# Attention scores and a token gather over three bfloat16 pieces in place of float32, with the exponentials one unit further behind

## The chip, the cores and the metric

The kernel runs on one core of a Trainium2 chip. The metric is the device time of one execution in microseconds (us), as the median of several runs. The core has five engines that run at the same time and wait for each other through semaphores: TensorE (PE in the profile; its weight loads are shown apart as PEld), VectorE (DVE), ScalarE (ACT), GpSimd (POOL) and SyncE (SP), which here only issues DMAs.

## The reference: what is computed

The input is x with 4 batches of 512 tokens of 128 numbers. In turn:

1. x = x + 0.5 * ffn(layernorm(x)), where ffn is a causal latent attention with 16 heads of 8 numbers, followed by a mixture of 8 experts of which 2 count for each token.
2. x = x + attention(layernorm(x)), a full (not causal) attention with 16 heads of 8 numbers.
3. Step 1 once more.
4. x = x + 0.5 * chosen(layernorm(x)): for each of 8 experts the 64 tokens with the highest gate are gathered, attend to each other with rotated positions, and are added back.
5. Four layers of additive attention with a feed-forward part, then step 4 once more.

Steps 1 to 3 are the "first layer" of the kernel. The scores of its attention are

```
scores = einsum('bhnd,bhmd->bhnm', q * scale, k)
attn = softmax(scores)
```

with only 8 numbers per head to sum over. All data are float32.

## The kernel before, in words

**Layout of the scores.** The attention of the first layer is 12 tasks: 3 parts (causal, full, causal) by 4 batches. A task keeps q and k transposed, spread over partitions so that a row group of 32 partitions (called j, 0 to 3) holds one head at every fourth partition, with 4 head groups g along the free dimension: tiles qA and kA (L240, L241), two of each, used in turn. A product of q's and k's rows of one row group sums over 32 partitions, of which 8 carry data. Partition 1 of every row group in kA is -1 and in qA is the maximum of that token's scores, so that the second product yields scores already less their maximum.

**Units.** A task is cut in units: a unit is a bank-wide (512 columns) piece of scores for one head group, 16 units in a full task and 10 in a causal one (there some units are made of two shorter pieces, 384+128 or 256+256 columns). There are 144 units. A unit is worked in two halves of two row groups each.

**Stages of a unit.** `maxima` (L522) multiplies q by k for tokens as rows; `reduce_max` (L536) takes the row maximum on VectorE (L543 with the causal mask, L547 without). When the last unit of a head group is reduced, `place_maxima` (L549) transposes the maxima on VectorE (L551) and puts them in qA's partition 1 by four DMAs (L555). GAP units later `shifted` (L557) multiplies k by q the other way round, `exponent` (L571) takes the exponential on ScalarE (L574), `mask` (L576) clears the upper triangle on GpSimd for causal tasks, and LAG units after that `products` (L590) multiplies by the values (L605).

**Order of the work.** The loop at L628 writes the order by hand. At step n it issues the maxima of unit n, the shifted scores of the unit that `behind` names (five units behind at first, FIRST; six after unit 26, HOLD and GAP at L22 and L23), the products two units later, and beside them one expert's `hidden` (L460) and one `combined` (L477) of the mixture, and one step of background work: the preparation of the next task (L301), its placing (L383), the ends of older ones. `bank` and `clock` (L53) choose a PSUM bank by planned times. A scheduler below this may still reorder what is independent.

**Preparing and placing a task.** `prepare` ends with q in qC (L346) and k in kC (L351), float32, 128 partitions by 512. `spread` (L354) copies both into qA and kA by one DMA each (for the first task by four each on two queues). It may run only when the task before last no longer reads the same buffers: L388 waits for the last unit of that task plus GAP.

**The gather.** `choice` (L778) computes the gates of two batches, finds the 64 highest per expert in eight rounds on VectorE (L836, L838), and leaves for each batch the token rows yg (the 128 normalised numbers, the rotation's cosines and sines, the place and the gates: 201 columns) and the slot numbers byt. `chosen_attention` (L858) builds a 0/1 matrix `pick` (L869) and multiplies it with yg (L880), 16 products per batch, which gathers the rows. It runs twice, after the first layer and after the additive layers; each time the choice for batches 2 and 3 runs while batches 0 and 1 are already attended to.

Of the kernel before, what the change touches and what calls it, by code (L numbers as in the profile page):

```python
# [21 lines left out]
FIRST, HOLD = 5, [26]  # L22
GAP, LAG = 6, 2  # L23
# [17 lines left out]
def tile_macaron(ctx: ExitStack, tc: tile.TileContext, a: dict, out: bass.AP):  # L41
# [55 lines left out]
    zeros = const.tile([4, T], F32, name="zeros")  # L97
# [134 lines left out]
    def first_layer(opened, picked):  # L232
        with (
# [6 lines left out]
            qAs = [hp.tile([P, NG, T], F32, name=f"qA{i}") for i in range(2)]  # L240
            kAs = [hp.tile([P, NG, T], F32, name=f"kA{i}") for i in range(2)]  # L241
# [3 lines left out]
            nc.vector.memset(qAs[0], 0.0)  # L245
            nc.vector.memset(kAs[0], -1.0)

            nms = [hp.tile([P, 32], F32, name=f"nm{g}") for g in range(NG)]
            for nm in nms:
                nc.gpsimd.memset(nm[:, 16:32], 0.0)  # L250
# [25 lines left out]
            class Task:  # L276
# [24 lines left out]
                def prepare(self):  # L301
# [43 lines left out]
                    self.qC = wp.tile([P, T], F32, name="qC", bufs=1)  # L345
                    nc.scalar.activation(self.qC, ps, AF.Copy, scale=HD**-0.5)  # L346
# [3 lines left out]
                    self.kC = wp.tile([P, T], F32, name="kC", bufs=1)  # L350
                    nc.scalar.copy(self.kC, ps)  # L351
                    self.ready = True

                def spread(self):  # L354


                    if self.k == 0:
                        for g in range(NG):
                            nc.sync.dma_start(self.qA[0:P:4, g, :], self.qC[g:P:4, :])
                            nc.scalar.dma_start(self.kA[0:P:4, g, :], self.kC[g:P:4, :])  # L360
                        return
                    if self.k > 1:
                        nc.sync.dma_start(self.qA[1:P:32], zeros[0:4, :].unsqueeze(1).to_broadcast([4, NG, T]))

                    nc.sync.dma_start(self.qA[0:P:4], self.qC)
                    nc.sync.dma_start(self.kA[0:P:4], self.kC)
# [143 lines left out]
            def attention():  # L510
# [11 lines left out]
                def maxima(n, j):  # L522
                    t, unit = units[n]
                    ps = bank((2.0 if len(unit) == 1 else 2.3) + (0.8 if len(unit) == 1 else 1.1) * (j % 2))
                    r0 = 32 * j
                    for g, c, at, w in unit:
                        nc.tensor.matmul(  # L527
                            ps[:, at : at + w],
                            lhsT=t.qA[r0 : r0 + 32, g, c * P : (c + 1) * P],
                            rhs=t.kA[r0 : r0 + 32, g, 0:w],  # L530
                            start=True,
                            stop=True,
                        )
                    return ps
# [14 lines left out]
                def place_maxima(t, g):  # L549
                    mT = wp.tile([P, 32], F32, name="mT")  # L550
                    nc.vector.transpose(mT, nms[g])  # L551

                    to = t.qA[1:P:32, g, :].rearrange("j (c u q) -> j c u q", c=NC, u=4)
                    for u in range(4):
                        nc.sync.dma_start(to[:, :, u, :], mT[32 * u : 32 * u + 16, :])  # L555

                def shifted(n, j, ps):  # L557
                    t, unit = units[n]
                    r0 = 32 * j
                    for g, c, at, w in unit:  # L560
                        q0, kc = first(t, c, w)
                        nc.tensor.matmul(  # L562
                            ps[:, at : at + w],
                            lhsT=t.kA[r0 : r0 + 32, g, kc * P : (kc + 1) * P],
                            rhs=t.qA[r0 : r0 + 32, g, q0:T],
                            start=True,
                            stop=True,
                        )
                    return ps
# [55 lines left out]
                for h0, h1 in zip(HOLD, HOLD[1:] + [len(units) + GAP]):  # L625
                    x0 = behind[-1] + 1
                    behind += [None] + list(range(x0, x0 + h1 - h0 - 1))
                for n in range(len(units) + GAP + LAG):  # L628
# [11 lines left out]
                    for part in range(2):  # L640
# [11 lines left out]
                        clock[0] += 1.1  # L652
                        for j, ps in zip(sj, sp):
                            reduce_max(s, j, ps)
                        for j, ps in zip(xj, xp):
# [103 lines left out]
            nc.vector.memset(qAs[1], 0.0)  # L759
            nc.vector.memset(kAs[1], -1.0)  # L760
# [17 lines left out]
    def choice(batches, done, top, picked):  # L778
# [4 lines left out]
        ygs = [top.tile([P, NC, YG], F32, name=f"m_yg{b}") for b in batches]  # L783
# [46 lines left out]
        for i in range(len(batches)):  # L830
            nc.gpsimd.tensor_copy(ygs[i][:, :, AT_G : AT_G + NE], gates[:, :, i * NE : (i + 1) * NE])
        yield
# [22 lines left out]
        for i, b in enumerate(batches):  # L855
            picked[b] = ygs[i], byt[:, :, i * NE : (i + 1) * NE]

    def chosen_attention(top, picked, choosing, beside=()):  # L858

        with tc.tile_pool(name="moa", bufs=2) as wp:  # L860

            def stream(b):

                yg, byt = picked[b]

                pick = wp.tile([P, NC, NE, KSEL], F32, name="pick")
# [8 lines left out]
                for k in range(2):  # L875
                    ps = bank().rearrange("p (i n) -> p i n", i=2)
                    for i in range(2):
                        r = 2 * k + i
                        for c in range(NC):
                            nc.tensor.matmul(  # L880
                                ps[:, i, 0:YG],
                                lhsT=pick[:, c, 2 * r : 2 * r + 2, :].rearrange("p e s -> p (e s)"),
                                rhs=yg[:, c, :],
                                start=(c == 0),
                                stop=(c == NC - 1),
                            )
# [77 lines left out]
                av = wp.tile([P, T], F32, name="av")  # L964
# [411 lines left out]
```

## Time and profile before

| | |
|---|---|
| median of 3 runs | 1371.02 us (1368.14 to 1375.04) |
| span of the profiled execution, first to last instruction | 1369.7 us |
| the profiled execution's own time around that span | not recorded in the page |
| PE busy, weight loads busy | 1289.1 us, 699.9 us |
| DVE, ACT, POOL busy | 954.4, 586.5, 562.1 us |
| mean granted clock of TensorE | 0.968 of full speed |
| score products for the maxima (L527), for the shifted scores (L562) | 349.0 us, 334.0 us of PE |
| products with the values (L605) | 183.7 us of PE |
| experts (L267) | 135.6 and 137.1 us of PE |
| gather (L880) | 51.0 us of PE |
| DMA | 39.52 MB, mean 29 GB/s |

Busy times are unions: where four products on four row groups run side by side, the time counts once. The trace shows the stages by where their lines start and end: the scores run from 17.4 us (first L527) to about 811 us (last L562); the experts of step 3 end near 888 us; the first gather starts at 888.8 us; the additive layers fill about 985 to 1256 us; the second gather starts at 1277.1 us; the rest is the end of the chosen attention and the output.

A group line of the page reads: line, engine, operation, output and input tiles, their sizes, number of records, then busy time, mean length in ns, the engine's idle time ahead of these records and what ended it. A waits line reads: who waited, for whom, total us, how many times, the longest.

### The profile page before, as it was taken

Reading aid. Unit: us, or ns where it says so; the run is one execution under the profiler, and the core shown is the slowest. Engines: PE = TensorE matmul, PEld = TensorE weight load, DVE = VectorE, ACT = ScalarE, POOL = GpSimd, SP = SyncE. Lnnn points to the kernel's source line nnn. Section 1 sums busy time; section 2 is a strip of 40 time slices with the busy share of each in tenths; the row PEclk is TensorE's granted clock in tenths of the full one; section 3 lists DMA queues with packets and bytes.
Section 4 is the critical chain, followed back from the end, with each engine's and each line's share of the span. In section 5 each row is a group of like instructions: output and inputs, shape, how many; then the busy total and the mean of one; then the engine's idle time right before and its main releaser. Section 6 shows DMA issues by size and latency. Waiting matters only on the chain. (4 is left out here: it accounts for less than half of the span.)

```text
span 1369.7 us, 29349 instructions
## 1 busy us (share of the span) xinstructions
PE 1289.1 (94%) x11050; PEld 699.9 (51%) x11050; DVE 954.4 (70%) x3293; ACT 586.5 (43%) x1180; POOL 562.1 (41%) x823
## 2 busy tenths in 40 slices
PE   5998999999999999999999999989889999997897
PEld 2554445333333333465544443367667767665675
DVE  6886776666658777778767638687466776667773
ACT  1555454454556666665545443222223332323222
POOL 8345655544424112024564755622244443543100
PEclk8999999999999999999999999999979999999799
DMA  3001101020111100000111011211000100000000
GB/s 115 21 24 41 43 33 49 2 80 1 64 45 32 39 1 18 3 19 19 50 33 34 33 53 28 76 40 40 1 20 5 40 1 17 1 1 1 1 9 23
DMA packets 37172, 39.52 MB, mean 29 GB/s; under 512 B 11080, under 2 KB 23880, under 8 KB 37032
## 3 DMA queue, kind: packets, MB, share of 16 engines
q1 hardware_dynamic: 34536, 35.06, 8.3%
q10 hardware_dynamic: 2496, 2.59, 0.6%
q8 instruction: 87, 1.43, 0.4%
q14 instruction: 53, 0.43, 0.1%
HBM read 29.45 MB, written 1.18 MB: 22 GB/s over the span
## 5 line engine op out<-in xcount | busy, mean ns | idle before, releaser
L574 ACT ACTIVATE e<-bank 128x512 f32<-128x512 f32 x576 | 313.7, 595 | 278.4 <-PE bank L527 240.0
L527 PE MATMUL bank<-kA,qA 32*128 32x512 f32 (+3 forms) x1536 | 349.0, 527 | 4.1 <-DVE nm L543 1.8
L562 PE MATMUL bank<-qA,kA 32*128 32x512 f32 (+3 forms) x1536 | 334.0, 524 | 0.3 <-DVE nm L543 0.3
L543 DVE CUSTOM_DVE_ANT_0 junk<-bank,causal 128x384 f32<-128x384 f32 (+3 forms) x512 | 251.0, 490 | 89.5 <-PE bank L527 51.3
L547 DVE TENSOR_REDUCE nm<-bank 128x1 f32<-128x512 f32 x256 | 164.9, 686 | 78.9 <-PE bank L527 78.7
L473 POOL TENSOR_TENSOR hid<-v,spread 128x512 f32<-128x512 f32 x128 | 163.9, 1286 | 127.1 <-DVE v L472 101.7
L562 PEld LDWEIGHTS bank<-qA,kA 32*128 32x128 f32 x1536 | 129.5, 185 | 136.9 <-issue 54.1
L605 PE MATMUL sum<-e,vA 128*32 128x256 f32 (+1 forms) x2560 | 183.7, 368 | 6.1 <-POOL e L580 6.0
L580 POOL TENSOR_SCALAR_AFFINE_SELECT e<-e 128x256 f32<-128x256 f32 x256 | 99.3, 407 | 192.8 <-ACT e L574 191.7
L527 PEld LDWEIGHTS bank<-kA,qA 32*128 32x128 f32 x1536 | 147.4, 187 | 24.6 <-DVE nm L543 5.8
L605 PEld LDWEIGHTS sum<-e,vA 128*32 128x32 f32 x2560 | 62.8, 109 | 165.8 <-issue 134.0
L267 PE MATMUL sum<-hid,sb_f_w 128*32 128x512 f32 x1024 | 135.6, 597 | 3.0 <-POOL hid L473 2.9
L267 PE MATMUL bank<-tT,sb_f_w 128*32 128x512 f32 x1024 | 137.1, 602 | 0.0
L472 DVE SCALAR_TENSOR_TENSOR v<-th,bank 128x512 f32<-128x512 f32 x128 | 87.0, 681 | 43.9 <-ACT th L467 29.2
L467 ACT ACTIVATE th<-bank 128x512 f32<-128x512 f32 x128 | 76.3, 597 | 49.0 <-PE bank L267 39.5
L154 POOL TENSOR_TENSOR r<-v,mhalf 128x4 f32<-128x4 f32 (+1 forms) x64 | 71.8, 1123 | 5.1
L1250 PE MATMUL bank<-h2T,w 128*128 128x512 f32 x128 | 69.0, 632 | 0.2 <-ACT h2T L1239 0.2
L1256 PE MATMUL bank<-w,hid 128*128 128x128 f32 x512 | 65.7, 277 | 0.1
L1256 PEld LDWEIGHTS bank<-w,hid 128*128 128x128 f32 x512 | 63.1, 194 | 4.8 <-issue 1.5
L1251 ACT ACTIVATE hid<-bank,sb_l_cols 128x512 f32<-128x512 f32 x64 | 43.9, 688 | 39.9 <-PE bank L1250 39.8
L1148 PE MATMUL bank<-wa,hT 128*128 128x385 f32 x128 | 56.5, 540 | 1.4 <-ACT hT L1141 1.4
L312 POOL TENSOR_SCALAR v<-mv 128x4 f32<-128x4 f32 x12 | 2.8, 230 | 131.1 <-DVE mv L171 130.8
(279 smaller groups left out, 1805.4 us busy)
## 6 DMA issues: line engine op xcount, KB each, us to landing
spread<-away SPq DMA_DIRECT2D x64, 256.0 KB
qA<-mT SPq DMA_DIRECT2D x192, 2.0 KB
qA<-qC SPq DMA_DIRECT2D x11, 256.0 KB
kA<-kC SPq DMA_DIRECT2D x11, 256.0 KB
w<-in_l_w_dram SPq DMA_DIRECT2D x8, 256.0 KB
sb_m_wqkv<-in_m_wqkv_dram SPq DMA_DIRECT2D x4, 384.0 KB
m_yg<-in_m_trig_dram SPq DMA_DIRECT2D x8, 130.0 KB
X<-in_x_dram SPq DMA_DIRECT2D x4, 256.0 KB
```

Of the source, the lines that this page charges most:

```text
L267: nc.tensor.matmul(ps[32 * j : 32 * j + 32, :], lhsT=w[:, 32 * j : 32 * j + 32], rhs=rhs, start=start, stop=stop, skip_group_check=True,)
L467: nc.scalar.activation(th, ph, AF.Tanh, scale=0.5)
L472: nc.vector.scalar_tensor_tensor(v, th, 1.0, ph, ALU.add, ALU.mult)
L473: nc.gpsimd.tensor_tensor(hid, v, self.spread[e], op=ALU.mult)
L527: nc.tensor.matmul(ps[:, at : at + w], lhsT=t.qA[r0 : r0 + 32, g, c * P : (c + 1) * P], rhs=t.kA[r0 : r0 + 32, g, 0:w], start=True, stop=True,
L543: nc.vector.tensor_tensor_reduce(junk[:, 0:w], src, causal[:, T - w : T], 1.0, NEG, ALU.add, ALU.max, dst)
L547: nc.vector.tensor_reduce(dst, src, axis=AX.X, op=ALU.max)
L562: nc.tensor.matmul(ps[:, at : at + w], lhsT=t.kA[r0 : r0 + 32, g, kc * P : (kc + 1) * P], rhs=t.qA[r0 : r0 + 32, g, q0:T], start=True, sto ...
L574: nc.scalar.activation(es[n][:, j, :], ps, AF.Exp)
L580: nc.gpsimd.affine_select(out=e, in_=e, pattern=[[0, 2], [1, P]], compare_op=ALU.is_ge, fill=0.0, base=0, channel_multiplier=-1,)
L605: nc.tensor.matmul(to[32 * j : 32 * j + 32, q0 + lo - at : q0 + hi - at], lhsT=t.vA[:, kc, 4 * j + g, :], rhs=es[n][:, j, lo:hi], start=fresh,
L1256: nc.tensor.matmul(pm[:, c * P : (c + 1) * P], lhsT=hid[:, f, c * P : (c + 1) * P], rhs=w2[:, f, :], start=(f == 0), stop=(f == 3),)
```

## The change

Every number that enters the scores is cut in three bfloat16 pieces: x0 is x rounded to bfloat16, x1 is the rounded rest, x2 what is left; their sum is the float32 number.

- **Scores.** k's three pieces take partitions 0, 1, 2 of every four in kA; the fourth stays -1. q's pieces are placed in three tiles qA[0], qA[1], qA[2], each rotated by one piece, so that the sum of three products (NS = 3 rounds) covers all nine pairs of pieces. Each float32 product of L527 and L562 becomes three bfloat16 products that add up in one bank. The rounds go over all four row groups of a half in turn (`in_rounds`).
- **Maxima.** They are cut in three pieces as well, by four small operations on GpSimd, and the transposed pieces go to the fourth partition of three of a row group's eight rows in qA[0].
- **Pieces of q and k.** ScalarE writes the first piece, VectorE subtracts it from the PSUM value, GpSimd makes the second and third piece.
- **Spread.** Twelve DMAs per task (three for k, nine for q) instead of two; the DMA of zeros now covers 16 rows.
- **Gather.** `pick` is bfloat16, GpSimd cuts the token rows in three pieces (`split`, after the gates are copied), and each product of L880 becomes three.
- **Order.** GAP is 7 instead of 6, with a second hold step at unit 27. The planned time of a half's scores is 0.7 instead of 1.1. The tile `av` shares the buffer of `xg`.

The core of the diff:

```diff
-FIRST, HOLD = 5, [26]
-GAP, LAG = 6, 2
+FIRST, HOLD = 5, [26, 27]
+GAP, LAG = 7, 2
+NS = 3
...
-            qAs = [hp.tile([P, NG, T], F32, name=f"qA{i}") for i in range(2)]
-            kAs = [hp.tile([P, NG, T], F32, name=f"kA{i}") for i in range(2)]
+            qAs = [[hp.tile([P, NG, T], BF16, name=f"qA{i}{r}") for r in range(NS)] for i in range(2)]
+            kAs = [hp.tile([P, NG, T], BF16, name=f"kA{i}") for i in range(2)]
...
+                def pieces(self, ps, scale, name):
+                    x = [wp.tile([P, T], BF16, name=f"{name}C{s}", bufs=1) for s in range(NS)]
+                    rest = wp.tile([P, T], F32, tag="v", name="rest")
+                    nc.scalar.activation(x[0], ps, AF.Copy, scale=scale)
+                    nc.vector.scalar_tensor_tensor(rest, ps, scale, x[0], ALU.mult, ALU.subtract)
+                    nc.gpsimd.tensor_copy(x[1], rest)
+                    nc.gpsimd.tensor_tensor(x[2], rest, x[1], op=ALU.subtract)
+                    return x
...
                     if self.k > 1:
-                        nc.sync.dma_start(self.qA[1:P:32], zeros[0:4, :].unsqueeze(1).to_broadcast([4, NG, T]))
-                    nc.sync.dma_start(self.qA[0:P:4], self.qC)
-                    nc.sync.dma_start(self.kA[0:P:4], self.kC)
+                        nc.sync.dma_start(self.qA[0][NS:P:8], zeros.unsqueeze(1).to_broadcast([16, NG, T]))
+                    moves = [(self.kA[s:P:4], self.kC[s]) for s in range(NS)]
+                    moves += [(self.qA[r][s:P:4], self.qC[(s + r) % NS]) for r in range(NS) for s in range(NS)]
+                    for i, (to, x) in enumerate(moves):
+                        (nc.scalar if self.k == 0 and i % 2 else nc.sync).dma_start(to, x)
...
+                    def product(r):
+                        for k, (g, c, at, w) in enumerate(unit):
+                            nc.tensor.matmul(
+                                ps[:, at : at + w],
+                                lhsT=t.qA[r][rows, g, c * P : (c + 1) * P],
+                                rhs=t.kA[rows, g, 0:w],
+                                start=r == 0 and k == 0,
+                                stop=r == NS - 1,
+                                skip_group_check=True,
+                            )
...
+                def in_rounds(*tiles):
+                    for r in range(NS):
+                        for _, product in tiles:
+                            product(r)
...
-                    mT = wp.tile([P, 32], F32, name="mT")
-                    nc.vector.transpose(mT, nms[g])
+                    m = nms[g].rearrange("p (j c) -> p j c", c=NC)
+                    split = pieces_of[g][:, :, 0:16].rearrange("p c (j s) -> p j s c", s=4)
+                    rest = wp.tile([P, 4, NC], F32, name="mR")
+                    nc.gpsimd.tensor_copy(split[:, :, 0], m)
+                    nc.gpsimd.tensor_tensor(rest, m, split[:, :, 0], op=ALU.subtract)
+                    nc.gpsimd.tensor_copy(split[:, :, 1], rest)
+                    nc.gpsimd.tensor_tensor(split[:, :, 2], rest, split[:, :, 1], op=ALU.subtract)
+                    mT = wp.tile([P, NC, 32], BF16, name="mT")
+                    nc.vector.transpose(mT, pieces_of[g])
...
-                        clock[0] += 1.1
+                        in_rounds(*xp, *sp)
+                        clock[0] += 0.7
...
+        def split(i):
+            for c in range(0, NC, 2):
+                x, of = [p[:, c : c + 2] for p in pieces[i]], ygs[i][:, c : c + 2]
+                rest = top.tile([P, T], F32, tag=f"yT{i}", name="rest")[:, 0 : 2 * YG].rearrange("p (c n) -> p c n", c=2)
+                nc.gpsimd.tensor_copy(x[0], of)
+                nc.gpsimd.tensor_tensor(rest, of, x[0], op=ALU.subtract)
+                nc.gpsimd.tensor_copy(x[1], rest)
+                nc.gpsimd.tensor_tensor(x[2], rest, x[1], op=ALU.subtract)
...
-                pick = wp.tile([P, NC, NE, KSEL], F32, name="pick")
+                pick = wp.tile([P, NC, NE, KSEL], BF16, name="pick")
...
+                            for k3, piece in enumerate(pieces):
+                                nc.tensor.matmul(
+                                    ps[:, i, 0:YG],
+                                    lhsT=pick[:, c, 2 * r : 2 * r + 2, :].rearrange("p e s -> p (e s)"),
+                                    rhs=piece[:, c, :],
+                                    start=(c == 0 and k3 == 0),
+                                    stop=(c == NC - 1 and k3 == 2),
+                                )
```

## The prediction

> **What bounds the kernel now.** I read the page first, then the busy time in stretches of 50 us, then the timeline inside three of them, then the waits there.
>
> From the page:
>
> ```profile
> PE 1289.1 (94%) x11050; PEld 699.9 (51%) x11050; DVE 954.4 (70%) x3293; ACT 586.5 (43%) x1180; POOL 562.1 (41%) x823
> ...
> L574 ACT ACTIVATE e<-bank 128x512 f32<-128x512 f32 x576 | 313.7, 595 | 278.4 <-PE bank L527 240.0
> L527 PE MATMUL bank<-kA,qA 32*128 32x512 f32 (+3 forms) x1536 | 349.0, 527 | 4.1 <-DVE nm L543 1.8
> L562 PE MATMUL bank<-qA,kA 32*128 32x512 f32 (+3 forms) x1536 | 334.0, 524 | 0.3 <-DVE nm L543 0.3
> ```
>
> PE looks full, but a busy PE need not be the bound. The two score lines (L527 for the maxima, L562 for the shifted scores) have 3072 records: the code has 1536 such products, so each float32 product is two records, each with its weight load. ACT's idle time is put down to PE. The timeline of one half unit of full attention, with no experts beside it:
>
> ```profile
> 478.65 0.70 PE L562 MATMUL bank<-qA,kA 32*128 32x512 f32 x2
> 478.66 0.79 PE L527 MATMUL bank<-kA,qA 32*128 32x512 f32 x2
> 479.18 0.59 PE L562 MATMUL bank<-qA,kA 32*128 32x512 f32 x2
> 479.80 0.16 PEld L605 LDWEIGHTS sum<-e,vA 128*32 128x32 f32 x8 [0.76 <-issue]
> 479.89 1.29 DVE L547 TENSOR_REDUCE nm<-bank 128x1 f32<-128x512 f32 x2 [0.41 <-PE bank L527]
> 480.37 0.19 PEld L562 LDWEIGHTS bank<-qA,kA 32*128 32x128 f32 x2 [0.41 <-issue]
> ```
>
> Columns are start, length, engine and line. Four products on four row groups run side by side: first records at 478.65, second at 479.18, the next kind (L605) at 479.80, the next half at 480.37. DVE needs 1.29 of that 1.72 us and waits 0.41 for PE. The stretches say the same by stage:
>
> ```profile
> 350.00:400.00 50.00, 50.00 (x480) 15.27 (x472) 29.35 (x47) 25.26 (x46) 22.45 (x20) 1.00 0.16 52
> 450.00:500.00 50.00, 50.00 (x463) 17.78 (x463) 38.03 (x70) 31.53 (x60) 8.32 (x11) 1.00 0.09 27
> 600.00:650.00 50.00, 48.05 (x540) 27.60 (x537) 41.62 (x172) 29.34 (x55) 19.71 (x44) 1.00 0.05 14
> 750.00:800.00 50.00, 50.00 (x524) 22.15 (x516) 28.12 (x97) 24.62 (x46) 36.12 (x53) 1.00 0.09 30
> ```
>
> The busy columns are PE, PEld, DVE, ACT, POOL, then the granted clock. Where the experts' products run beside attention (100 to 405 and 650 to 810) PE is the bound and DVE has room. In full attention alone (405 to 555) PE is still the bound, with DVE close behind. In causal attention alone (27 to 100, 555 to 650) DVE is: its masked maxima fill it, and its wait for PE is small:
>
> ```profile
> DVE junk L543 <- PE bank L527: 4.5, 8, 1.3
> ```
>
> That is over 560 to 640: 4.5 us in 80.
>
> **The change part by part.** All sums are against the profiled execution, whose span is 1369.7 us. What lies around that span is not in the profile; the median of the three runs is 1371.0, so 1.3 us are added at the end.
>
> *Scores, the gain.* In steps free of waits a float32 record takes 0.107 us per 128 columns: at 610.84 and 610.94 two 128-column records follow by 0.10, and 256-column ones at 613 by 0.21. So 512 columns take 0.427, two records 0.853, and the 1.07 us from the first score to L605 (401.72 region: 469.90 to 470.97) leave 0.10 for the first load and 0.11 before the next kind starts. The bfloat16 product is shown only by this:
>
> ```profile
> L932 PEld LDWEIGHTS <-ident_h x32: 95/100/101, 909.3 to 1352.1; 128*128 128x128 bf16 x32
> L932 PE MATMUL bank<-paired,ident_h x32: 218/219/230, 909.4 to 1352.2; 128*128 128x128 bf16 x32
> ```
>
> Its load takes 100 ns against 184 to 190 for float32. Load and product together advance PE by about 0.12 us (0.335 from 909.45 to 909.78, less two float32 records). [...] Three rounds are 0.64 against 0.853, and with the same 0.21 around them a half takes 0.85 instead of 1.07: **0.22 saved**. This needs the loads of the next round to hide under the running one; the float32 trace shows it (second loads at 470.01, under records that run to 470.43). In causal halves a 128-column piece is shorter than its load (0.053 against 0.10), so 384+128 takes 3 x 0.26 = 0.78, the others 0.64; with seven units between the two streams three of five pairings contain such a unit, mean 0.72, so **0.17 saved** of 1.10. Ends: nothing saved if loads show fully (3 x 0.31 + 0.11 = 1.04), 0.27 if they vanish.
>
> [...]
>
> How many halves: of 288, the reductions and exponentials in the stretches give 46 full and 81 causal beside experts, 82 full alone, 79 causal alone. PE-bound ones: 46 x 0.22 + 81 x 0.17 + 82 x 0.22 = 10 + 14 + 18 = 42. DVE does not clip this: in full attention alone it is busy 37 of 50 us at 1.85 us a half, 1.37, and PE comes down to 1.63. The 79 causal ones give what DVE waited for PE, about 5. **Gain 47.**
>
> *Gather.* 128 products (L880) become 384. A float32 one is two records of 0.168 (22 in 3.71 us), 0.335; three bfloat16 ones are bound by their 0.10 loads, 0.30. 128 x 0.035 = 4.5; PE is only part of those stages' path, so **3** (0 to 10).
>
> *Pieces of q and k.* Per task, twice: DVE's subtraction from PSUM (like L472, 0.68), POOL's copy (L831 0.212 at 32 columns, the cast at L112 0.279 at 128, so about 0.55 at 512) and subtraction (L473, 1.28). At the start nothing covers them. q is ready at 13.67, then 0.68 + 1.83 to 16.2; k's pieces follow on POOL to 18.0, or 19.8 behind a 1.8 us memset (L256); then the last of the twelve DMAs, 0.58 each, on two queues. The first maxima came at 17.4: **5 later** (3 to 8). Later the POOL part hides behind attention. DVE's 1.36 us per task counts where DVE is the bound, for some 4 tasks: **6**.
>
> *Spread.* Two DMAs (three with zeros) become twelve or thirteen on SP, at 0.57 each 7.4 us instead of 1.7. With GAP 7 they start one unit later, seven units into the task before: of ten causal units 2.5 are left, 11 us, into which must also go four maxima DMAs (2.3). Six tasks are so tight; **6** in all (0 to 20). In full tasks nine units are left.
>
> *Maxima.* Four small POOL operations (about 0.2 each, L681), a wider transpose on DVE (0.21 now; up to 0.4), then the same four DMAs. Behind the waiting transpose stand the next reductions. One unit more of GAP gives 3 to 4.5 us against some 1.5: nothing. The first 26 units keep five: **3** (0 to 10), also because the spread of task 1 is ahead of them on SP.
>
> *Split in the choice.* Per batch two chunks of two copies (0.47) and two subtractions (1.03): 6 us, 12 for two batches, all on POOL and issued ahead of what POOL does next. The first lies beside experts' work, covered. The others come before the additions at L921, L892 and L1266, which the last streams wait for; DVE's sixteen-odd us of top-eight rounds cover part: **6** (0 to 20).
>
> *Hold, memsets, tail.* The second hold only shifts exponentials; the last unit of lag runs beside PE-bound expert work: nothing, at most 3. The memsets are ahead of q at the start and take about what they took.
>
> Sum: 47 + 3 - 5 - 6 - 6 - 3 - 6 = **24 saved**: span 1345.7, time **1347**.
>
> **The rivals.**
> 1. *Loads in front of every round (slower).* If the twelve loads of a half do not hide under bfloat16 products half as long as float32's, a half takes 1.04 and the 42 shrink to about 6; 26 of costs remain less the gather's 3: 1387. For: the only bfloat16 row alternates and shows its load. Against: loads on four row groups start within 20 ns and overlap today. It decides when less than about 0.11 is saved per half. **0.18.**
> 2. *The queues take it.* SP's 7.4 us per task and POOL's added 130 us (562 now) delay the maxima, so that the exponentials wait for qA: half the gain goes, or costs are double: 1360 to 1376, middle 1368. For: POOL is busy 36 of 50 us at 750. Against: six units were ample, waits for these DMAs total 4 us. **0.20.**
> 3. *All of it shows.* Loads vanish (0.27 a half in both kinds, 56), costs at their low ends (3 + 6 for DVE and the start, little else), gather 5: about 50 saved, 1320. **0.20.**
> 4. Row groups that do not overlap in bfloat16 would cost over a microsecond a half, far out: 0.02.
>
> **How the numbers follow.** The forecast, 1335 to 1360, has 0.40. The range goes to rivals 3 and 1: 1312 to 1388. A measurement of this kernel can tell 0.5%, 7 us: faster holds the forecast, rival 3 and a third of rival 2, 0.67; the same the rest of it and edges, 0.14; slower 0.19.
>
> **What would show it.** Right: L527 and L562 as bfloat16 records of 32x512, 4608 together; in full attention alone a half from 1.72 to about 1.5 us, DVE's wait for L527 gone to under 0.2; a step of about 0.21 between rounds; first maxima near 22 us. Wrong: rounds 0.3 apart (rival 1); ACT or PE waiting for qA<-mT or kA by tens of us (rival 2); causal stretches that lengthen because of DVE's subtraction; last stage longer with POOL busy after 1256.

## The result, and the profile after

The changed kernel takes 1470.5 us (median of 4 runs, 1468.7 to 1473.0) against 1369.6 beside it: a ratio of 1.073, interval 1.070 to 1.076. The prediction was 1347, with a range to 1388. The span went from 1369.7 to 1466.9 us. From the page and the groups of the kernel after (line, engine, operation, busy us and mean ns, then the idle time ahead of it and what ended it):

```profile
PE 1253.2 (85%) x12714; PEld 645.8 (44%) x12714; DVE 973.2 (66%) x3321; ACT 585.0 (40%) x1180; POOL 695.6 (47%) x1127
...
L541 PE MATMUL bank<-kA,qA 32*128 32x512 bf16 (+3 forms) x2304 | 294.4, 347 | 77.4 <-DVE nm L564 35.9 <-DMA kA<-kC 22.7 <-DVE rest L364 6.7
L593 PE MATMUL bank<-qA,kA 32*128 32x512 bf16 (+3 forms) x2304 | 278.6, 343 | 31.5 <-DVE nm L568 17.5 <-DVE nm L564 6.3 <-DVE rest L364 4.9
...
L580 DVE STREAM_TRANSPOSE mT<-mp 128x128 bf16<-128x128 bf16 x48 | 15.0, 311 | 80.5 <-POOL mp L578 80.2 <-DMA qA<-qC 0.3
```

The products did get shorter: L541 and L593 (L527 and L562 before) take 573 us of PE in place of 683. But PE fell from 94% to 85% of a longer span. It now waits 109 us ahead of these two lines (23 of them once, at the start), 4.4 before, and DVE waits 80 us at the transpose of the maxima (L580) for POOL. One half of full attention, where nothing is late, shows the product itself:

```profile
500.67 0.39 PE L593 MATMUL bank<-qA,kA 32*128 32x512 bf16 x2
...
500.90 0.38 PE L593 MATMUL bank<-qA,kA 32*128 32x512 bf16 x2
...
501.11 0.38 PE L593 MATMUL bank<-qA,kA 32*128 32x512 bf16 x2
...
501.47 0.64 PE L638 MATMUL sum<-e,vA 128*32 128x256 f32 x8
...
502.04 0.39 PE L593 MATMUL bank<-qA,kA 32*128 32x512 bf16 x2
```

Rounds start 0.21 to 0.23 apart, the scores take 0.80 us to the next kind of product (forecast 0.85, before 1.07), and the next half starts after 1.37 us where before it took 1.72. The gain is there, but 1.37 is an undisturbed half: from exponential to exponential, the halves of the units in full attention alone (60 to 103) have a median of 1.84 us and a mean of 2.13, against 1.77 and 1.90 before. What eats the gain is seen 26 us later in the same stage:

```profile
527.04 3.13 POOL L343 TENSOR_SCALAR Y<-X,mv,r 128x128 f32<-128x128 f32 x4
530.12 0.25 POOL L575 CAST mp<-nm 128x16 bf16<-128x16 f32 x1
530.46 0.23 POOL L576 TENSOR_TENSOR mR<-nm,mp 128x16 f32<-128x16 f32 x1
530.75 0.25 POOL L577 CAST mp<-mR 128x16 bf16<-128x16 f32 x1
531.09 0.27 POOL L578 TENSOR_TENSOR mp<-mR,mp 128x16 bf16<-128x16 f32 x1
531.39 0.31 DVE L580 STREAM_TRANSPOSE mT<-mp 128x128 bf16<-128x128 bf16 x1 [5.99 <-POOL mp L578]
531.63 1.85 DVE L568 TENSOR_REDUCE nm<-bank 128x1 f32<-128x512 f32 x3
531.77 1.21 SPq L584 DMA_DIRECT2D qA<-mT  x2
532.33 0.61 PE L593 MATMUL bank<-qA,kA 32*128 32x512 bf16 x2 [4.80 <-DVE nm L568]
```

Read it downwards. The maxima of a group are ready, but POOL is at the next task's normalization (3.13 us). Then the four pieces take 1.24 us. DVE stands at the transpose for 5.99 us, and its next instructions are the reductions that free PSUM banks, so PE stands 4.80. The exponentials that need this maximum come seven units later: in the whole trace neither ACT nor PE waits for a DMA qA<-mT. Over all 48 transposes, 36 of the 80 us lie before POOL starts the first piece (POOL's queue) and 44 after that (the four pieces, one after the other).

The start is the second place. The first maxima in the kernel before, then POOL and the first maxima in the kernel after:

```profile
17.36 3.13 PE L527 MATMUL bank<-kA,qA 32*128 32x512 f32 x28 [0.90 <-DMA kA<-kC]
```

```profile
14.69 3.54 POOL L263 MEMSET vA<- 128x2048 f32 x2
...
21.13 0.62 POOL L365 CAST qC<-rest 128x512 bf16<-128x512 f32 x1
...
26.27 3.15 POOL L330 TENSOR_SCALAR h<-X,mv,r 128x128 f32<-128x128 f32 x4
29.40 3.13 POOL L343 TENSOR_SCALAR Y<-X,mv,r 128x128 f32<-128x128 f32 x4
...
34.80 0.61 POOL L365 CAST kC<-rest 128x512 bf16<-128x512 f32 x1
...
39.55 2.94 PE L541 MATMUL bank<-kA,qA 32*128 32x512 bf16 x29 [22.72 <-DMA kA<-kC]
```

q's rest is there at 15.5 and k's at 17.2, but the constants and then the second task's `prepare` are ahead of their pieces on POOL. The first maxima come at 39.6 instead of 17.4. By the first exponential of a unit, after runs 22 us behind before at unit 0, 56 at unit 24, 40 at unit 60 (between these two experts run beside attention, PE is the bound and the gain shows), 82 at unit 124; 86 at the first gather, 97 at the end.

### The profile page after: what moved, and what is told of

Its sections match the earlier page's. It is cut to its first block, busy times and chain, and to the rows that moved or that the text cites. A ratio compares the mean times of both kernels' runs of the same rounds, so it can differ in the third digit from the quotient of the medians.

```text
span 1466.9 us, 33148 instructions
## 1 busy us (share of the span) xinstructions
PE 1253.2 (85%) x12714; PEld 645.8 (44%) x12714; DVE 973.2 (66%) x3321; ACT 585.0 (40%) x1180; POOL 695.6 (47%) x1127
## 5 line engine op out<-in xcount | busy, mean ns | idle before, releaser
L541 PE MATMUL bank<-kA,qA 32*128 32x512 bf16 (+3 forms) x2304 | 294.4, 347 | 77.4 <-DVE nm L564 35.9
L593 PE MATMUL bank<-qA,kA 32*128 32x512 bf16 (+3 forms) x2304 | 278.6, 343 | 31.5 <-DVE nm L568 17.5
L638 PE MATMUL sum<-e,vA 128*32 128x256 f32 (+1 forms) x2560 | 194.6, 388 | 9.3 <-POOL e L613 9.3
L593 PEld LDWEIGHTS <-kA 32*128 32x128 bf16 x2304 | 91.4, 95 | 223.4 <-issue 201.6
L541 PEld LDWEIGHTS <-qA 32*128 32x128 bf16 x2304 | 104.4, 96 | 95.7 <-issue 82.3
L274 PE MATMUL bank<-tT,sb_f_w 128*32 128x512 f32 x1024 | 141.3, 615 | 2.8 <-DVE v L484 2.3
L580 DVE STREAM_TRANSPOSE mT<-mp 128x128 bf16<-128x128 bf16 x48 | 15.0, 311 | 80.5 <-POOL mp L578 80.2
L575 POOL CAST mp<-nm 128x16 bf16<-128x16 f32 x48 | 12.3, 256 | 103.6 <-DVE nm L568 74.7
```

The lines of the kernel that those rows point to most:

```text
L274: nc.tensor.matmul(ps[32 * j : 32 * j + 32, :], lhsT=w[:, 32 * j : 32 * j + 32], rhs=rhs, start=start, stop=stop, skip_group_check=True,)
L541: nc.tensor.matmul(ps[:, at : at + w], lhsT=t.qA[r][rows, g, c * P : (c + 1) * P], rhs=t.kA[rows, g, 0:w], start=r == 0 and k == 0, stop=r ...
L593: nc.tensor.matmul(ps[:, at : at + w], lhsT=t.kA[rows, g, kc * P : (kc + 1) * P], rhs=t.qA[r][rows, g, q0:T], start=r == 0 and k == 0, sto ...
L638: nc.tensor.matmul(to[32 * j : 32 * j + 32, q0 + lo - at : q0 + hi - at], lhsT=t.vA[:, kc, 4 * j + g, :], rhs=es[n][:, j, lo:hi], start=fresh,
```

## The experiments

Behind each time stands its ratio to the kernel before on the same chip, with a 95% interval. The groups of runs below ran on several chips, on which the kernel before took 1369.4 to 1371.2 us, so a difference between groups is uncertain by some 2 us.

### The three parts that went to POOL

In maxima_on_vector and first_on_vector:

```diff
-                    nc.gpsimd.tensor_copy(split[:, :, 0], m)
+                    nc.vector.tensor_copy(split[:, :, 0], m)
...
-                    nc.gpsimd.tensor_copy(x[1], rest)
-                    nc.gpsimd.tensor_tensor(x[2], rest, x[1], op=ALU.subtract)
+                    eng = nc.gpsimd if self.k else nc.vector
+                    eng.tensor_copy(x[1], rest)
+                    eng.tensor_tensor(x[2], rest, x[1], op=ALU.subtract)
```

(The other three lines of the maxima's cut change in the same way.) gather_undone takes `split` and the pieces out of `choice` and gives `pick` and yg in float32 to the gather; it keeps the change's shared buffers of yg and `av`. all_three makes the three edits.

> The changed kernel with one edit: the four small operations that cut a group's maxima into pieces (L575 to L578) run on DVE instead of POOL. Theory A (POOL's queue): DVE stands at the transpose L580 for pieces that wait on POOL behind a next task's prepare, 80 us in all in the trace of after, and the reductions and PE's banks stand behind it. Without the trip to POOL these waits go, DVE takes some 25 us more of small operations, and 60 to 80 us come back: 1390 to 1410. Theory B (SP's queue: twelve or thirteen DMAs per task delay the maxima's own DMAs): the maxima are cut sooner but land no sooner, and the time stays within 10 us of 1470. Theory C (the granted clock is lower because the bfloat16 score products run denser, and that alone costs the time): the waits go but the clock stays near 0.91, and no more than 30 us come back: 1440 or more.

> The changed kernel with one edit: for the first task alone the second and third pieces of q and k are cut on DVE instead of POOL. Theory A (POOL's queue): at the start the cast of q waits on POOL behind the constants to 21.1 us and that of k behind the next task's prepare to 34.8, so the first maxima come at 39.6 instead of 17.4. On DVE they come at 22 to 25, and 13 to 17 us come back in all: 1454 to 1458. Theory B (the twelve spread DMAs on two queues are what the first maxima wait for): the first maxima come at 33 or later and less than 7 us come back.

> The changed kernel with the second part of the change undone: the chosen tokens are gathered in float32 again, with no split on POOL. Theory A (POOL's queue): the two splits delay what POOL does next by 10 to 12 us in the experts' tail and again in the last stage; the gather's own gain on PE is 12 us of busy time of which a few count. Undone, 12 to 22 us come back: 1448 to 1458. Rival (the split lies beside other work, as the prediction had it, and the gather's gain counts): the time stays within 5 us of 1470 or rises.

> The three edits together: maxima cut on DVE, the first task's pieces on DVE, the gather in float32. What is left of the change is the three-piece scores, seven units instead of six, the spread's DMAs, and the pieces of q and k of the later tasks on POOL. Theory A (POOL's queue): the three parts add up, 90 to 115 us come back, 1355 to 1380, at or somewhat below the kernel before. Theory B (SP's queue and its DMAs): most of the loss stays, 1430 or more. Theory C (the clock): the clock stays near 0.91 and the time stays above 1400.

Measured: maxima_on_vector 1431.7 (1.045, 1.042 to 1.049), first_on_vector 1458.5 (1.064, 1.061 to 1.066), gather_undone 1455.0 (1.061, 1.058 to 1.064), and all_three 1408.1 (1.027, 1.024 to 1.029). That is 39, 12, 15.5 and 62 us back: each part is real and they nearly add up, but theory A was too simple. It left 38 us over before, and the maxima gave 39 instead of 60 to 80. The twelve spread DMAs per task are still in all_three, so theory B falls as an account of most of the loss. The granted clock rose as the time fell (0.913 to 0.935), so theory C falls too; whether the lower clock costs something by itself is taken up with the filler below.

### What is left in the attention

one_piece adds to all_three that the reductions write one bfloat16 maximum themselves:

```diff
-                        dst = nms[g][:, NC * j + c : NC * j + c + 1]
+                        dst = pieces_of[g][:, c, 4 * j : 4 * j + 1]
```

and has no cutting of pieces in `place_maxima`. The three others change one thing more in it: `GAP, LAG = 6, 2` and `HOLD = 5, [26]`; the rounds of a half

```diff
-                    for r in range(NS):
-                        for _, product in tiles:
-                            product(r)
+                    for r in range(NS + 1):
+                        for i, (_, product) in enumerate(tiles):
+                            at = r - (i == 3)
+                            if 0 <= at < NS:
+                                product(at)
```

and two filling products into the kept bank ahead of `in_rounds`. In this order they are one_piece_gap6, one_piece_stagger and one_piece_filler.

> The three edits together, and besides the maximum is given to the scores as one bfloat16 number instead of three pieces: the reductions write bfloat16 themselves, so that the four small operations per group are gone altogether (the rows of the other two pieces stay zero; the softmax is the same, since all keys of a query are shifted by the same number). The three edits left 38 us over the kernel before. Theory A2 (what is left in the causal stages is DVE's own work: four operations of about 0.2 us for 48 groups, 37 us of DVE, and half of them where DVE is the bound): 18 to 30 us less than with the three edits, 1378 to 1390. Rival D (the granted clock: with the bfloat16 scores PE waits more for DVE, its clock falls to a half, and then PE is the bound): at most 10 us less, 1398 or more.

> As the one-piece kernel, with the exponentials six units behind and one hold, as before the change. Theory G (the seventh unit costs nothing and gives nothing, as the prediction had it): within 5 us of the one-piece kernel. Rival: the seventh unit is needed for the spread's DMAs, and with six the exponentials wait for the maxima's rows: more than 7 us slower than the one-piece kernel; or it only makes the last stage longer, and six are 5 us or more faster.

> As the one-piece kernel, but in the rounds of a half the last of the four tiles runs one round behind the other three. Theory S (the rounds run the four tiles in lockstep, so that one tile whose PSUM bank is still being reduced holds up the next rounds of all four, exponentials included: in full attention alone a half takes 1.78 us where it waits and 1.40 where not): the late tile has 0.22 us more, and 8 to 25 us go. Rival (the wait only moves, and the added fourth step of 0.2 us shows in the 288 halves): 10 to 50 us slower than the one-piece kernel.

> As the one-piece kernel, with two more bfloat16 products of 512 columns (0.43 us at full clock) in front of each half's scores in the causal stages without experts' products; they add some 1e-30 to the sums, nothing that counts, and only keep PE busy where it would wait for DVE. Theory D (the granted clock falls to a half after PE's waits for DVE, and a causal half then takes 2.4 us instead of 1.7): the clock in the stretches 30 to 140 and 560 to 670 stays above 0.95 and 10 to 25 us go. Rival (the clock is no bound there, DVE is): the time is the same or up to 20 us longer by the added products.

Measured: one_piece 1379.5 (1.006, 1.004 to 1.009), one_piece_gap6 1370.2 (0.999, 0.997 to 1.001), one_piece_stagger 1373.6 (1.002, 1.000 to 1.003), one_piece_filler 1388.8 (1.014, 1.011 to 1.018).

- Without the four small operations on DVE 28.5 us go, in the range of A2. In all_three their medians are 0.19 to 0.23 us, as expected, but single ones take up to 1.3 us, and their records add up to 60 us, not 37.
- Six units and one hold are 9 us better than seven and two; which of the two edits it is was not taken apart.
- The filler raised the clock and lost 9 us. The stretches 55 to 120 and 560 to 660, first of one_piece, then of the filler kernel (busy us of PE, PEld, DVE, ACT, POOL, then the granted clock):

```profile
55.00:120.00 65.00, 56.46 (x810) 24.80 (x810) 50.98 (x210) 32.54 (x60) 27.47 (x59) 0.87 0.12 34
560.00:660.00 100.00, 82.95 (x1166) 40.55 (x1159) 72.86 (x291) 49.73 (x92) 37.27 (x75) 0.86 0.12 36
```

```profile
55.00:120.00 65.00, 59.12 (x822) 24.13 (x821) 48.31 (x202) 30.45 (x57) 22.98 (x52) 0.94 0.12 34
560.00:660.00 100.00, 89.55 (x1267) 41.04 (x1260) 75.96 (x301) 51.42 (x96) 38.75 (x76) 0.97 0.13 36
```

Theory D, that 10 to 25 us would go, falls. But its condition held in the later stretch alone (over 30 to 140 us the clock was 0.86, not 0.95), and the filler is not free: 160 products of some 0.21 us are 34 us of PE, by estimate. What the low clock costs by itself is therefore not shown; nothing here says that it is more than a trace of PE's waits.

- The late tile gained 6 us, less than the 8 to 25 of theory S. What it relieves, in full attention in one_piece:

```profile
481.23 0.39 PE L586 MATMUL bank<-qA,kA 32*128 32x512 bf16 x2
481.23 0.09 PEld L541 LDWEIGHTS <-qA 32*128 32x128 bf16 x2
481.24 0.84 PE L541 MATMUL bank<-kA,qA 32*128 32x512 bf16 x2
481.71 0.09 PEld L586 LDWEIGHTS <-kA 32*128 32x128 bf16 x2 [0.38 <-issue]
481.71 0.39 PE L586 MATMUL bank<-qA,kA 32*128 32x512 bf16 x2
...
482.42 1.29 DVE L568 TENSOR_REDUCE mp<-bank 128x1 bf16<-128x512 f32 x2 [0.49 <-PE bank L541]
```

Two L541 products stand in one line that begins at 481.24 and is 0.84 long, so the second began about 0.45 late; round two starts at 481.71, 0.48 after round one instead of 0.22. One tile that waits for a bank (the previous half's reductions ran to 481.93, its exponentials to 481.66) holds all four, and DVE then waits 0.49 for PE. Halves from exponential to exponential between 410 and 545 us have a median of 1.78 us in one_piece and 1.61 with the late tile, where undisturbed ones take 1.3 to 1.45. So the wait for one tile is real, but it is a small part of the loss.

### More of the order, and the gather by itself

c_stagger is one_piece with six units, the late tile, and a buffer of its own for `av`. c_stagger2 has `at = r - (i >= 2)`. c_pairs runs, in causal stages without experts, `in_rounds(*xp)` and then `in_rounds(*sp)`. only_gather16 is the kernel before with the change's second part alone (`split`, the bfloat16 gather and the shared buffers).

> The repairs found so far together: one bfloat16 maximum written by the reductions, the first task's pieces on DVE, the gather in float32 with the buffers of the kernel before (the attended values of the chosen tokens in a buffer of their own again, where the change had let them share that of the gathered tokens), six units and one hold, and the last tile of a half one round late. Theory (the gains of six units, 9 us, and of the late tile, 6, add up, and the shared buffer is what made the last stage 8 us longer from the second gather to the end although its code is otherwise that of before): 1370 less 6 less 8, 1350 to 1360, faster than the kernel before by 1%. Rival (the last stage is longer for another reason, and the late tile gains only where the seventh unit loses): 1364 to 1372.

> As c_stagger, but both maxima tiles of a half run one round behind the two shifted ones, so that the exponentials' products do not stand behind a maxima tile whose bank is still being reduced. Theory S (lockstep over PSUM banks): as fast as c_stagger or up to 10 us faster. Rival (the fourth step shows in every half): 5 to 15 us slower than c_stagger.

> As c_stagger, but in the causal stages without experts the three rounds of the shifted scores run first and those of the maxima after them, two tiles side by side instead of four. Theory S (in the causal stages DVE's reductions set the pace, and the lockstep of exponentials and maxima is what lost 10 us in units 0 to 16 and 6 to 14 in units 100 to 124 against the kernel before): 5 to 15 us faster than c_stagger. Rival (two tiles side by side take twice PE's time, 1.3 us instead of 0.66, and that decides): 5 to 25 us slower.

> The kernel before with the second part of the change alone: the chosen tokens gathered over three bfloat16 pieces that POOL cuts, the attended values sharing the gathered tokens' buffer. Theory A (POOL's queue, the split delays POOL's other work): 8 to 18 us slower than before, as undoing it in the changed kernel gave 15. Rival (as the prediction had it, 3 us slower: 6 for the split less 3 for the gather; or the 15 us came only from the crowded POOL of the whole change): within 4 us of before.

Measured: c_stagger 1365.6 (0.996, 0.994 to 0.997), c_stagger2 1364.5 (0.996, 0.994 to 0.997), c_pairs 1361.0 (0.994, 0.992 to 0.996), and only_gather16 1394.0 (1.017, 1.015 to 1.020).

The second late tile of c_stagger2 gives nothing that shows. The separate rounds of c_pairs give 4.5 us, just short of theory S, and their intervals overlap; by the traces the experts end 3 us earlier, and the rest is in the stages behind them, where the edit does nothing.

c_stagger missed its 1350 to 1360: the shared `av` was not what lengthened the last stage, which was still 100.8 us from the second gather to the end, as in one_piece_gap6 (92.6 before). The trace of c_stagger shows what is:

```profile
1271.22 0.38 PE L195 MATMUL bank<-ident,xs 128*128 128x128 f32 x2
1271.42 1.12 DVE L184 TENSOR_SCALAR m_yg<-X,mv,r 128x128 f32<-128x128 f32 x4 [2.16 <-PE bank L908]
1271.44 0.51 PE L908 MATMUL bank<-m_yg,pick 128*128 128x201 f32 x2
1271.45 11.45 SPq L813 DMA_DIRECT2D m_yg<-in_m_trig_dram  x2
```

The next choice's L184 and its DMA stand until the gather (L908) has read m_yg, since the change numbers these buffers so that two choices share them. My undoing of the gather had kept that name. The second part by itself costs 23 us, above both theories: more than in the full change (15.5), where the undoing carried the cost of the shared buffers.

### Buffers, and what of the gather's 23 us is the split

d_buffers is c_pairs with

```diff
-        ygs = [top.tile([P, NC, YG], F32, name=f"m_yg{i}") for i in range(len(batches))]
+        ygs = [top.tile([P, NC, YG], F32, name=f"m_yg{b}") for b in batches]
```

d_pairs_all drops the condition on experts from c_pairs' order. split_alone is the kernel before with `split` called where the change calls it, its results unused; it also lets `av` share the buffer of `xg`, as the change does. d_gather16 is c_pairs with the change's gather and its shared `av`.

> As c_pairs, with the source rows of the gather in a buffer for each pair of experts' batches again, as before the change (the change had numbered them so that a later choice takes the same two buffers; in the last stage of c_stagger DVE's L184 and a DMA of the next choice then stand behind the gather). Theory: those waits go, the stage from first gather to additive layers falls from 105 to 96 us and the last stage from 97 to 93, and the time is 1346 to 1352. Rival (the stages are longer because the whole program's order and PSUM banks differ): within 4 us of c_pairs, 1357 to 1365.

> As d_buffers, but shifted scores first and maxima after them in all causal stages, beside experts too. Theory S (the lockstep over PSUM banks costs in every causal half): 3 to 10 us faster than d_buffers. Rival (beside experts PE is the bound, and two tiles side by side take 0.6 us more of PE per half, in 80 halves): 15 to 50 us slower.

> The kernel before with the split on POOL alone: POOL cuts the chosen tokens' source rows into pieces at the same place, but nothing uses them and the gather is that of before. Theory A (the split delays what POOL does next, in the experts' tail and at the second choice): 14 to 22 us slower than before, nearly all of the 23 that the whole second part costs. Rival (the split is covered and the bfloat16 gather itself, or its wait for the last piece, costs): within 6 us of before.

> As c_pairs, but with the gather of the change (three bfloat16 pieces cut on POOL): what is left of the change against the kernel before is then all of it but the pieces of the maximum, the first task's pieces on POOL, the seventh unit and the order of the rounds. Theory A: the split costs here as it does alone, 10 to 23 us over c_pairs, 1371 to 1384. Rival (the shared buffers of c_pairs cost 8 to 10 us which the pieces avoid, so that the split nearly pays): 1358 to 1368.

Measured: d_buffers 1350.0 (0.986, 0.984 to 0.987), d_pairs_all 1353.2 (0.987, 0.986 to 0.989), split_alone 1393.7 (1.018, 1.017 to 1.019), d_gather16 1373.0 (1.002, 1.001 to 1.003).

d_buffers is 1.4% faster than the kernel before. The first chosen stage fell from 104.8 to 97.7 us, the last from 96.8 to 94.1. d_pairs_all is the same within the runs, both its theories missed. split_alone costs all that the second part costs, 24 us; the bfloat16 gather gives nothing that shows. The shared `av` is in these 24 us too, but in c_stagger a buffer of its own for `av` left the last stage as long as it was, so the split is the likely cause of nearly all of them. d_gather16 is 12 us over c_pairs, in theory A's range, and 23 over d_buffers. split_alone at the end of the experts:

```profile
846.77 0.90 POOL L795 TENSOR_TENSOR m_p<-rest,m_p 128x402 bf16<-128x402 f32 x1
847.62 0.95 POOL L793 TENSOR_TENSOR rest<-m_yg,m_p 128x402 f32<-128x402 f32 x1
848.51 0.52 POOL L792 CAST m_p<-m_yg 128x402 bf16<-128x402 f32 x1
...
851.04 1.27 POOL L473 TENSOR_TENSOR hid<-v,spread 128x512 f32<-128x512 f32 x1
...
852.36 1.93 PE L267 MATMUL sum<-hid,sb_f_w 128*32 128x512 f32 x8 [5.35 <-POOL hid L473]
```

The split's operations have the lengths forecast (0.52 and 0.95), but they stand between the experts' own products on POOL (L473), and PE stands 5.35 us for one of these. The last experts' product ends 9.7 us later than before. At the second choice the same pieces hold the addition that the last normalization needs: from last additive layer to second gather 57.6 us instead of 53.3. The other 10 us are in the two stages of chosen attention (99.5 us instead of 95.9, and 99.0 instead of 92.6); what they wait for was not taken apart.

### Queue or chain: the maxima's trip over POOL again

Both are d_buffers with one thing put back: the reductions write float32, and one copy on POOL (e_one_pool), or the change's four operations (e_four_pool), stand ahead of the transpose.

> As d_buffers (1350), but the reductions write float32 and one small copy on POOL makes the bfloat16 maximum ahead of DVE's transpose. Theory Q (the queue: the copy waits behind a next task's normalization and masks on POOL, 36 us in the trace of after, and DVE stands behind it in its own order): 20 to 45 us slower than d_buffers. Theory C (the four operations' own 1.24 us are what costs, a single one of 0.25 us is nearly free): 5 to 15 us slower.

> As d_buffers, but with the change's three-piece maximum and its four operations on POOL; so all that is left repaired is the seventh unit, the gather, the first task and the order of the rounds. Theory Q: not more than 20 us over the kernel with one operation on POOL. Theory C: 40 to 60 us over it. By the trace of after (48 x 1.24 us of chain, 36 us of queue) the whole is 60 to 80 us over d_buffers, 1410 to 1430.

Measured: e_one_pool 1391.5 (1.015, 1.013 to 1.017) and e_four_pool 1430.5 (1.044, 1.042 to 1.046): 41.5 us over d_buffers for one small copy, 39 for the other three. (d_buffers ran on another chip; by the ratios it is 40 and 40.) DVE's waits in the first and the second (who waited, for whom, us, times, longest):

```profile
DVE mT L579 <- POOL mp L577: 66.2, 39, 11.4
```

```profile
DVE mT L583 <- POOL mp L581: 109.7, 47, 12.4
```

Both theories hold half: the trip with one copy costs about as much as three more operations in it. A single copy of 0.25 us takes 66 us of DVE's time because of what it stands behind: 55 of them lie before POOL starts the copy, most of them in `prepare`'s normalization and the masks. In e_four_pool it is again 55 for the queue, and 56 for the chain.

## Why the prediction was wrong, point by point

- **Scores: the product right, its gain in part by luck.** 0.85 us forecast, 0.80 measured. No run shows by itself the 0.213 us for a bfloat16 product of 512 columns, or the 0.053 for 128, that the forecast counted with; what the kernel after shows is rounds that start 0.21 to 0.23 us apart, also where one holds a unit of 384+128 columns (0.22, from 616.66 to 616.88), for which 0.26 was forecast. Loads hide: those of the second round, 0.09 us at 500.72, run under the first round's records (0.39 us from 500.67). Rival 1 did not come. From the first exponential to the last experts' product the kernel before takes 847.7 us and d_buffers 817.2, 30.5 less. My terms for that stretch (47 less 6 for DVE's subtraction, 6 for the spread, 3 for the maxima) give 32, near it, though d_buffers has another order of rounds and one maximum piece. Stage by stage it is less near. From the first exponential of one unit to that of another, d_buffers gains 10 us in units 20 to 40 and 11 in 40 to 60, beside experts, but only 9 in 60 to 104 (88 halves), full attention alone, where 18 were forecast for 82 halves ("DVE does not clip this": the mean half came to 1.79 us, not 1.63). In the causal stages alone, where "about 5" were to come, units 104 to 124 gain 3 and units 0 to 20 lose 11.
- **Maxima: the step that failed, a wait priced for the wrong party.** "Behind the waiting transpose stand the next reductions" was written down, and then priced by what the exponentials can wait: "One unit more of GAP gives 3 to 4.5 us against some 1.5: nothing", 3 us. GAP is slack for those who need the result. It is none for the engine that stands in front of the transpose. Each operation was nearly right (0.2 forecast, 0.23 to 0.27 measured), and so were the 1.5 us (1.24), but they come 48 times in DVE's own order, and the queue ahead on POOL (`prepare`'s 3.1 us blocks) was not counted. Measured instead of the 3 us: 80 us when put on d_buffers; in the changed kernel 39 came back when the operations moved to DVE, and 28.5 more (on all_three) when they went.
- **Split: size right, cover wrong.** 12 us of POOL's work were forecast and are there. "The first lies beside experts' work, covered": the experts' products need POOL themselves, each 1.28 us, one after the other. 24 us instead of 6, with the shared `av` in it.
- **Start: too short.** "5 later" counted the operations and one memset, not all the constants and the next task's `prepare` that the order puts ahead; 22 us at the first maxima, 12 at the end of the run. With the first task's pieces on DVE it is 7.7 (first maxima at 25.1).
- **Rounds: not seen.** That four tiles in rounds share the wait of the one whose PSUM bank comes last was no part of the sum; 6 us for the late tile, and 3 to 4.5 more for separate rounds in causal stages, hardly clear of the noise.
- **Shared buffers: not seen.** The shared m_yg cost 9 to 11 us when the gather was float32. In the change itself the gather reads the pieces and not m_yg, so this wait should not be there; the last stage fits that, 96.3 us in the change and 100.8 in gather_undone.
- **Gap and hold.** "Nothing, at most 3" was forecast; going back to six units and one hold gained 9 us.
- **Spread, and DVE's subtraction: open.** No experiment took either out. d_buffers has both and is still 1.4% faster than before, and apart from the start its trace shows only some 2 us of waits for these DMAs; but what it loses in units 0 to 20 is not explained.
- **Rival 2** had POOL's 130 us right (562 to 696), but named the exponentials as those who wait, and ended at 1376. The waiting party was DVE, and through it PE.

d_buffers comes to 1350 us where 1347 was forecast, but that is luck: it leaves out the maxima's pieces and the split, and has orders that the forecast did not know. The parts measured one by one (80, 24, 12, 9 and some 10 for the rounds) are 135 us, between d_buffers and the change there are 120: they overlap somewhat.

## What to carry to other kernels

A small operation is priced by three things: its length, what its engine has queued ahead of it, and what stands behind whoever waits for it, in that engine's own order. A hand-over to another engine in the middle of a full queue can cost that round trip each time, however much slack the result's user has: here 41.5 us of 66 us of waits showed in the time. No trip at all, by letting the reduction write the type that is wanted, beat every trip that was tried (1350.0 us against 1391.5 and 1430.5); a transpose placed later in DVE's order, when the pieces are ready, was not tried. When an edit is undone to price it, its side effects (a shared buffer) must be undone too.

## What the runs showed of the hardware

In all_three the granted clock fell behind a stretch in which PE was mostly idle (busy us of PE, PEld, DVE, ACT, POOL, then the clock):

```profile
97.50:100.00 2.50, 0.89 (x12) 0.27 (x9) 2.22 (x7) 0.41 (x1) 0.41 (x1) 1.00 0.06 16
100.00:102.50 2.50, 2.50 (x45) 1.18 (x40) 1.75 (x7) 1.20 (x3) 0.41 (x1) 0.68 0.07 7
102.50:105.00 2.50, 2.50 (x42) 0.94 (x40) 1.73 (x9) 1.17 (x3) 0.77 (x2) 0.63 0.51 167
```

PE is busy 0.89 us of the first 2.5, at a clock of 1.00; in the next two stretches, where it is busy throughout, the clock is 0.68 and 0.63. What made it fall was not tested. In the kernel after, rounds of four products start 0.21 to 0.23 us apart (500.67, 500.90, 501.11), 53 to 58 ns for each product with its load.
